# One planner for projection pieces and results, by the latest half each allows

## The chip, the cores and the metric

One NeuronCore of a Trainium2 chip runs the whole kernel. The metric is the device time of one execution in microseconds; three executions of the kernel before gave 4173.58, 4173.59 and 4175.78 us, median 4173.59 us. Everything is float32 except the row maxima that are turned into bfloat16 triples.

## The reference

The input x is (4, 2048, 512). It is layer-normalized to xn; the output is x plus an attention over xn plus a top-1 mixture of experts over xn.

```python
qkv = x @ w_qkv                                   # 512 -> 3 x 512
q, k = spectral_filter(q), spectral_filter(k)     # rfft over the 32 head entries, mask, irfft
scores = einsum('bhqd,bhkd->bhqk', q, k) / sqrt(32)
out = einsum('bhqk,bhkd->bhqd', softmax(scores), v)   # 16 heads, 2048 queries, 2048 keys
attention = out.reshape(B, S, 512) @ w_out + b_out
# experts: each token picks argmax of softmax(xn @ w_gate); the first 100 tokens of each of 8
# experts get gate * (xn @ w_expert + b_expert), all others nothing
x + attention + experts
```

The spectral filter is linear, so it is folded into the weights of q and k once at the start. Attention over 4 x 16 heads of 2048 x 2048 scores is nearly all of the work.

## The kernel before

The work is cut into 16 groups `k` (batch k // 4, four heads each), a group into 4 blocks `n` of 512 queries, a block into 16 *halves* `j` of 128 keys. There are 1024 halves, numbered h = 64 k + 16 n + j; the place of a half in its block is h mod 16. Two halves are a window. The main loop goes through the halves in order, and every engine's instructions keep the order in which they are written (class `InOrder`, whose line 82 is why nearly all instructions of the profile carry L82).

Each half does the same base work:

- TensorE computes two pieces of scores for the *row maxima*, which run 21 halves ahead (`max_matmuls`, four PSUM banks of 128x512 a half, profile name `array<-keys,q`), and the scores themselves by adding the difference between neighbouring key tiles to what PSUM still holds (`scores`, `array<-q,steps_of_keys`).
- ScalarE exponentiates the four score banks in two instructions into the tiles `even` or `odd`.
- VectorE reduces the four banks of the maxima (`max_reduce`, `part<-array`). The first two banks always take one instruction each; the last two take one common instruction if the half's planned cost is above zero, and two otherwise (the argument `u == 0 or not costs[...]` in the main loop).
- TensorE multiplies the *previous* half's exponentials by v (`products`, `array<-even,v` and `array<-odd,v`), and VectorE adds the result to `num`.
- GpSimd and a DMA that accumulates add the exponentials of pairs of halves for the row sums, once a window.

After `products` the half runs its *agenda*: a list of further steps that was planned before the loop. What stands there:

- **Pieces**: `query_key` and `value` compute q, k and v of the next group, 128 tokens at a time: 48 pieces for a group, each 32 matmul instructions of 128 columns (`array<-xnT,w` for q and k, `array<-w,xnT` for v) and one ScalarE copy to q, keys or v. The first piece after a block of maxima is complete also carries the transpose of those maxima (`max_turn`).
- **Closing a block** (`close_steps`): at 5 halves after a block's end a `fold` of row sums on TensorE, at 6 to 13 one of eight reciprocals each on VectorE (`invert`), at 14 a GpSimd product `ot`, then four `result` steps (8 matmuls against w_out each, copied to y by ScalarE, or added to b_out by VectorE in groups with k mod 4 = 0), then `add`, a GpSimd-issued DMA that accumulates 1 MB of y into the output. Before, the results stand at 17, 18, 19, 20 and `add` at 21 halves after the block's end, always.
- **Weight loads** (`load_qkv_weights`): the three weight tiles of the next-but-one group, one buffer each for q, k and v, so each load stands one half after the last piece that uses the old weights. SyncE issues them.
- In the last group of a batch (k mod 4 = 3, except the last) the next batch's tokens: loads of x into `xs`, 16 normalizations on ScalarE (`xs<-xs`), 16 `turn` steps (transposes on TensorE and a ScalarE copy to xnT), then the routing of the tokens to experts (`plan_route`). In group 13 the experts themselves (`place_experts`).

Costs in the plan are counted in pieces: a piece, a result or a fold is 1, a turn 0.5, an expert step up to 5 (`at`, line 927).

Before, the pieces of group k + 1 are placed by `spread` (line 931) within group k alone. It takes an order written out by hand (`projections`, line 468, with two groups named in `CROWDED`), and looks for the lowest even level of cost at which the order fits into the group's 64 halves. The results are already in `costs`, at their fixed halves, and `spread` fills around them as an accumulated sum. The k pieces have an earliest half (the old keys must have been read, `SPENT`, line 1066) and a latest one (the maxima of the next group read them), passed as `latest`.

Of the kernel before, what the change touches and what calls it, by code (L numbers as in the profile page):

```python
# [26 lines left out]
NT = S // P  # L27
# [13 lines left out]
WIN = 2  # L41
NW = NT // WIN
MAX_AHEAD = 42
CROWDED = (1, (B - 1) * NG + 2)


def shape_constants():
# [54 lines left out]
def attention_and_top1_experts(ctx: ExitStack, tc: tile.TileContext, a: dict, out: bass.AP):  # L102
# [304 lines left out]
    def load_qkv_weights(k, s):  # L407
        wg[k, s] = weights.tile([P, NR, P], F32, name=f"w{s}", bufs=1)
        cols = slice(2 * DM + k % NG * P, 2 * DM + (k % NG + 1) * P)
        on.sync.dma_start(out=wg[k, s], in_=w_qkv[:, :, cols] if s == 2 else wd[k % NG][:, :, s, :])  # L410
# [54 lines left out]
        on.scalar.copy(vs[k][:, n * TQ + first : n * TQ + last, :], done)  # L465
        max_store(turned)

    def projections(k, tiles=1, kinds=None):

        kinds = [] if kinds is None else kinds  # L470

        if k == 0:
            order = [(query_key, 0, 1), (query_key, 0, 0)]
            order += [(query_key, n, 1) for n in range(1, NQ)] + [(query_key, 1, 0)]
            order += [(value, n) for n in range(NQ)] + [(query_key, n, 0) for n in range(2, NQ)]
        else:
            first = 2 if k in CROWDED else 3 if k % NG == 0 else 4
            queries, vals = ([(f, n, *s) for n in range(NQ)] for f, *s in ((query_key, 0), (value,)))
            news = [(query_key, n, 1) for n in range(NQ)]
            if first == 4:  # L480
                order = vals + queries[:2] + news + queries[2:]
            else:
                order = vals[:first] + queries[:1] + news[:3]
                order += vals[first : first + 1] + news[3:] + vals[first + 1 :] + queries[1:]
        kinds.extend((2 if f is value else at[1]) for f, *at in order for t in range(0, TQ, tiles))
# [221 lines left out]
    def close_steps(k, n):  # L707

        b = k // NG
        held = {}  # L710

        def fold():
            held["den"] = work.tile([P, QB], F32, tag="den", name="den", bufs=1)
            held["factor"] = work.tile([P, QB], F32, tag="factor", name="factor", bufs=1)
            on.scalar.copy(held["den"], row_sums(ended[k, n][1]))

        def invert(i):
            at = slice(i * PART, (i + 1) * PART)
            on.vector.reciprocal(held["factor"][:, at], held["den"][:, at])

        def divide():
            held["ot"] = work.tile([P, QB], F32, tag="ot", name="ot", bufs=1)
            engine = on.vector if (k, n) == (B * NG - 1, NQ - 2) else on.gpsimd
            engine.tensor_tensor(held["ot"], ended[k, n][0], held["factor"], ALU.mult)

        def result(t):
            if t == 0:
                held["y"] = chunk("y")
            if k % NG == 0:
                on.vector.tensor_tensor(held["y"][:, t, :], project(k, held["ot"], t), b_out, ALU.add)  # L730
            else:
                copy = on.vector.tensor_copy if k == B * NG - 1 and n > 0 else on.scalar.copy
                copy(held["y"][:, t, :], project(k, held["ot"], t))

        def add():
            on.gpsimd.dma_start(out=o[b, n], in_=held["y"], accum_op=ALU.add)

        if (k, n) == (B * NG - 1, NQ - 2):
            steps = [(5, 2, fold)] + [(6 + i // 3, 0, invert, i) for i in range(QB // PART)]
            steps += [(9, 0, divide)]  # L740
            first = 10
        else:
            steps = [(5, 1, fold)] + [(6 + i, 0, invert, i) for i in range(QB // PART)]
            first = 17
            heads[(k * NQ + n + 1) * HB + 14].append(divide)
        steps += [(first + t, 1, result, t) for t in range(TQ)]
        return steps + [(first + TQ, 0, add)]

    def close_last(k, n, num, tiles, y):

# [180 lines left out]
    def spread(steps, last, latest={}):  # L931


        base = steps[0][1]

        def places(level):
            half, done, found = base, costs[base], []
            for place, (cost, first, _) in enumerate(steps):
                stop = latest.get(place, last + 1)
                while half < stop and (half < first or done + cost / 2 > level * (half - base + 1)):  # L940
# [8 lines left out]
        found = next(filter(None, (places(level / 32) for level in range(16, 400))))  # L949
        for (cost, _, step), half in zip(steps, found):  # L950
            at(half, step, cost=cost)
        return found

    stage = {}

# [3 lines left out]
    def in_stage(which, *args):  # L959
        stage["all"][which](*args)  # L960
# [28 lines left out]
    def plan(k):  # L989
# [1 line left out]
        b, c = divmod(k, NG)  # L991
        start = k * GH

        def after_keys_are_spent():

            for i, place in enumerate([j for j, s in enumerate(kinds) if s == 1]):
                cost, _, step = steps[place]
                steps[place] = cost, start + SPENT + i // TQ * TQ, step
                latest[place] = start + SPENT + i // TQ * TQ + 3 * TQ - 1
# [7 lines left out]
        last = start + GH - 1  # L1007
        steps, kinds, latest = [], [], {}
        if k == 0:
            done = spread([(1, 0, step) for step in first_projections_left], 15)  # L1010
            for s in range(3):
                at(done[-1] + 1, load_qkv_weights, 1, s)
            plan_route(20, lambda i: first_route[i]())
            ready = done[-1] + 3
        if c == NG - 2 and b + 1 < B:

            at(start + 20, begin_stage, b + 1)
# [10 lines left out]
        pieces = projections(k + 1, kinds=kinds)  # L1028
        if c == NG - 1:

            late = {8: 9, 12: 14}
            order = [("turn", i) for i in range(8)] + pieces[:4] + [("turn", i) for i in range(8, 12)]
            order += pieces[4:8] + [("turn", i) for i in range(12, NT)] + pieces[8:]
            kinds = [None] * 8 + kinds[:4] + [None] * 4 + kinds[4:8] + [None] * 4 + kinds[8:]
            steps, first = [], start + 1
            for step in order:
                if isinstance(step, tuple):
                    i = step[1]
                    steps.append((0.5, start + late[i] if i in late else 0, lambda i=i: in_stage(4, i)))
                else:  # L1040
                    steps.append((1, 0, step))
            steps[0] = (0.5, first, steps[0][2])
            after_keys_are_spent()
            done = spread(steps, last, latest)
            turned = {i: done[order.index(("turn", i))] for i in range(NT)}
            for i in range(NT):
                at(turned[i] - 1, in_stage, 3, i)
# [3 lines left out]
        else:  # L1051
            steps = [(1, ready if k == 0 else start, step) for step in pieces]
            after_keys_are_spent()
            done = spread(steps, last, latest)
        assert done[-4] >= start + 3 * HB and done[-8] >= start + 2 * HB
        places = [[h for h, s in zip(done, kinds) if s == kind] for kind in range(3)]
        for i, h in enumerate(places[1]):
            assert SPENT <= h - start - i // TQ * TQ < SPENT + 3 * TQ
        assert places[0][3] < start + GH - MAX_AHEAD // 2 and places[0][7] < start + GH + HB - MAX_AHEAD // 2
        for n in range(NQ):  # L1060
            at(start + GH - 10 + n * TQ, key_steps, n)
        if k + 2 < B * NG:
            for s in range(3):
                at(places[s][-1] + 1, load_qkv_weights, k + 2, s)

    SPENT = GH - HB - MAX_AHEAD // 2 + TQ
    ROUTE = len(first_route)
# [12 lines left out]
    place_experts((B - 1) * NG * GH)  # L1080
    for k in range(B * NG):
        plan(k)

    FINAL = (B * NG * NQ - 1) * NW
    LEFT = 3
# [154 lines left out]
```

## Time and profile before

The profiled execution took 4171.94 us, of which 4170.1 us are the span from the first to the last instruction of the program.

| what | value |
|---|---|
| median of three runs | 4173.59 us |
| profiled execution, its span | 4171.94 us, 4170.1 us |
| TensorE matmul busy | 4135.3 us (99%) |
| VectorE busy | 3421.8 us (82%) |
| GpSimd busy | 3010.8 us (72%) |
| ScalarE busy | 2490.8 us (60%) |
| granted TensorE clock | 0.999 of full speed |
| reduces of one bank (128x512) | 2162, 685 ns each |
| reduces of two banks (128x1024) | 967, 1217 ns each |

Engine busy time is the union of instruction intervals. Matmuls overlap one another and their ends are modelled, so two matmul intervals can touch although the array waited between them; the distance between the *starts* of neighbouring groups of matmuls is safer. In this text the length of a half is the distance from the start of its `products` matmuls to the start of the next half's; the agenda of a half lies inside its own length. `PE` is TensorE's matmuls, `DVE` VectorE, `ACT` ScalarE, `POOL` GpSimd, `SP` SyncE.

### The profile page before, as it was taken

What the parts mean: (1) busy time and instruction counts of PE and PEld (TensorE: products, weight loads), DVE (VectorE), ACT (ScalarE), POOL (GpSimd) and SP (SyncE); (2) the same over time, 40 slices, a digit from 0 to 9 for tenths busy, and PEclk for the clock granted to TensorE, in tenths of its full rate; (3) what the DMA queues carried; (4) which work ended last, traced back from release to release, by engine and by line L of the source; (5) the groups of instructions that cost most, each with busy time, mean ns of one, the idle gap of its engine ahead of it and who ended that gap; (6) DMA issues with size and microseconds to landing.
All of it is one profiled execution on the core that took longest, in us unless ns stands there. A gap on an engine that the chain in (4) does not pass through costs nothing.

```text
span 4170.1 us, 121446 instructions
## 1 busy us (share of the span) xinstructions
PE 4135.3 (99%) x52824; PEld 1839.8 (44%) x52824; DVE 3421.8 (82%) x4940; ACT 2490.8 (60%) x3430; POOL 3010.8 (72%) x2102
## 2 busy tenths in 40 slices
PE   8999999999999999999999999999999999999999
PEld 5444444444444444444444444444444443444432
DVE  7778888977888888897788888888778888788895
ACT  4555556676665566657565556566656555556665
POOL 1578776776876777776778767767678776677887
PEclk9999999999999999999999999999999999999999
DMA  3677878987788788899778787899877986778787
GB/s 123 141 154 151 168 149 170 219 195 145 146 164 159 152 161 159 193 198 195 140 149 162 158 160 151 163 198 202 173 154 146 182 159 134 151 160 170 152 169 154
DMA packets 178415, 680.78 MB, mean 163 GB/s; under 512 B 23430, under 2 KB 53288, under 8 KB 113112
## 3 DMA queue, kind: packets, MB, share of 16 engines
q0 software_dynamic: 109856, 601.63, 74.0%
q1 hardware_dynamic: 67952, 71.34, 5.2%
q8 instruction: 414, 6.78, 0.6%
q14 instruction: 121, 0.99, 0.1%
q10 hardware_dynamic: 72, 0.03, 0.0%
HBM read 71.07 MB, written 87.91 MB: 38 GB/s over the span
## 4 chain that ended last, share of the span: by engine, by line
PE 94%; DVE 4%; ACT 1%; issue 1%; DMA 0%; SPq 0%; ACTq 0%
PE array L82 94%; DVE part L82 3%; DVE num L82 1%; ACT odd L82 0%; DVE factor L82 0%; DMA odd<-in_L_attn_w_qkv_dram 0%; DMA w<-in_L_attn_w_qkv_dram 0%; ACT even L82 0%; ACT keys L82 0%; SPq L82 0%; DVE stats L82 0%; DVE y L82 0%; ACT xnT L82 0%; ACT xs L82 0%; SPq L177 0%
## 5 line engine op out<-in xcount | busy, mean ns | idle before, releaser
L82 DVE TENSOR_REDUCE part<-array 128x1 f32<-128x512 f32 (+1 forms) x3129 | 2484.4, 850 | 667.6 <-PE array L82 662.8
L82 POOL TENSOR_TENSOR even<-even 128x1024 f32<-128x1024 f32 x876 | 2121.2, 2521 | 430.6 <-DMA even<-odd 422.9
L82 PE MATMUL array<-keys,q 32*128 32x512 f32 x8192 | 2059.3, 614 | 15.8 <-DVE part L82 5.8
L82 PE MATMUL array<-q,steps_of_keys 32*128 32x512 f32 x8128 | 2021.2, 615 | 0.1
L82 ACT ACTIVATE odd<-array 128x1024 f32<-128x1024 f32 x1024 | 996.7, 1021 | 472.2 <-PE array L82 403.5
L82 ACT ACTIVATE even<-array 128x1024 f32<-128x1024 f32 x1014 | 984.7, 1021 | 440.7 <-PE array L82 425.7
L82 PEld LDWEIGHTS array<-keys,q 32*128 32x128 f32 x8192 | 771.5, 184 | 580.5 <-DVE part L82 351.6
L82 PEld LDWEIGHTS array<-q,steps_of_keys 32*128 32x128 f32 x8128 | 689.2, 183 | 241.3 <-issue 227.9
L82 POOL DMA_DIRECT2D even<-odd x504 | 463.9, 920 | 336.3 <-ACT odd L82 300.2
L82 DVE TENSOR_TENSOR num<-num,array 128x512 f32<-128x512 f32 x960 | 651.0, 678 | 32.7 <-PE array L82 31.3
L82 PEld LDWEIGHTS array<-xnT,w 128*32 128x32 f32 x16384 | 458.7, 110 | 259.6 <-DVE part L82 177.6
L82 PE MATMUL array<-odd,v 128*32 128x512 f32 x4096 | 545.5, 605 | 0.0
L82 PE MATMUL array<-even,v 128*32 128x512 f32 x4056 | 540.2, 605 | 0.8 <-DVE part L82 0.8
L82 PE MATMUL array<-xnT,w 128*32 128x128 f32 x16384 | 527.4, 273 | 2.8 <-issue 1.7
L82 PEld LDWEIGHTS array<-w,xnT 128*32 128x32 f32 x8192 | 229.8, 110 | 147.8 <-DVE part L82 105.0
L82 DVE RECIPROCAL factor<-den 128x64 f32<-128x64 f32 x504 | 274.7, 546 | 0.0
L82 PE MATMUL array<-w,xnT 128*32 128x128 f32 x8192 | 269.4, 273 | 1.9 <-DMA w<-in_L_attn_w_qkv_dram 1.7
L82 PE MATMUL array<-wo,ot 128*32 128x512 f32 x2048 | 266.1, 592 | 0.0
L82 PEld LDWEIGHTS array<-odd,v 128*32 128x32 f32 x4096 | 80.7, 108 | 387.6 <-DVE part L82 379.8
L82 PEld LDWEIGHTS array<-even,v 128*32 128x32 f32 x4056 | 79.8, 108 | 385.3 <-DVE part L82 380.8
L82 POOL DMA_DIRECT2D out_dram<-y x63 | 87.3, 1385 | 176.9 <-ACT y L82 108.5
L82 ACT COPY q<-array 128x128 f32<-128x128 f32 x256 | 67.9, 265 | 182.1 <-PE array L82 178.3
(152 smaller groups left out, 1529.8 us busy)
## 6 DMA issues: line engine op xcount, KB each, us to landing
even<-odd POOLq DMA_DIRECT2D x504, 1024.0 KB, 8.1
out_dram<-y POOLq DMA_DIRECT2D x63, 1024.0 KB, 9.6
xs<-in_L_attn_x_dram SPq DMA_DIRECT2D x96, 256.0 KB
out_dram<-in_L_attn_x_dram SPq DMA_DIRECT2D x16, 1024.0 KB
w<-wd SPq DMA_DIRECT2D x30, 256.0 KB
w<-in_L_attn_w_qkv_dram SPq DMA_DIRECT2D x16, 256.0 KB
wo<-in_L_attn_w_out_dram SPq DMA_DIRECT2D x16, 256.0 KB
negm<-row SPq DMA_DIRECT2D x192, 4.0 KB
```

What stands on the lines that cost most here:

```text
L82: done = act(*args, **kwargs)
```

## The change

All pieces and results go into four queues (`jobs`): q, k, v pieces and results, each in a fixed order, over the whole kernel. An entry holds the earliest half (`release`), the latest (`stop`), the least distance to the entry before it in its queue, the step, and what is to follow one half later (the weight load after the last piece of a kind, or `add` after the last result). A new planner, `level`, goes through the halves once from first to last. A half whose cost is under 0.6 takes the ready entry with the nearest `stop`. A half that has something already takes more only if an entry's `stop` is this very half, or if a look ahead over 48 halves (`missed`) says that waiting would make an entry late.

So pieces of group k + 1 may now stand in group k + 1 itself: v pieces up to three halves before their product, q pieces of later blocks up to 22 halves before the block. Results may slip by up to 8 halves (by 1 in groups with k mod 4 = 0). `CROWDED`, the order by hand and `latest` go. The first piece of a kind stands at least 5 halves after the last piece of that kind of the group before; the weight load between them stands 4 halves or more ahead of it (3 in group 0, where it stands at half 16 and the first piece at 19). In the last group of a batch `spread` still places the turns, against a template of pieces. Within a half the pieces and results now come after all other agenda steps.

The same steps run with the same operands. The planned cost of the halves is 1152.75 before and after. Halves (of 1024) with a planned cost of 0 or 0.25: 84 before, 33 after; with 2 or 2.25: 130 before, 98 after. The program of the changed kernel has the same instructions on every engine, but for 96 one-bank reduces that become 48 two-bank ones on VectorE.

```diff
-CROWDED = (1, (B - 1) * NG + 2)
...
+            order = [(query_key, n, 0) for n in range(NQ)] + [(query_key, n, 1) for n in range(NQ)]
+            order += [(value, n) for n in range(NQ)]
...
-        steps += [(first + t, 1, result, t) for t in range(TQ)]
-        return steps + [(first + TQ, 0, add)]
+        results = [lambda t=t: result(t) for t in range(TQ)]
+        if k == B * NG - 1 and n > 0:
+            steps += [(first + t, 1, step) for t, step in enumerate(results)] + [(first + TQ, 0, add)]
+        else:
+            end = (k * NQ + n + 1) * HB
+            spare = 1 if k % NG == 0 else 8
+            for t, step in enumerate(results):
+                jobs[3].append((end + first, end + first + t + spare, 5 if t == 0 else 1, step, add if t == TQ - 1 else None))
+        return steps
...
+    jobs = [[] for _ in range(4)]
+
+    def level(first, last):
+
+        done = [[] for _ in jobs]
+
+        def ready(half, placed):
+
+            found = []
+            for q, (queue, before) in enumerate(zip(jobs, placed)):
+                if len(before) < len(queue):
+                    release, stop, gap, *_ = queue[len(before)]
+                    if half >= release and (not before or half >= before[-1] + gap):
+                        found.append((stop, q))
+            return min(found, default=None)
...
+        for half in range(first, last):
+            load = costs[half]
+            while found := ready(half, done):
+                stop, q = found
+                if load >= 0.6 and stop > half:
+                    if load > 1.8:
+                        break
+                    tried = [before + [half] if p == q else before for p, before in enumerate(done)]
+                    if missed(half, tried) >= missed(half, done):
+                        break
+                done[q].append(half)
+                load += 1
+        for queue, found in zip(jobs, done):
+            assert len(queue) == len(found)
+            for (release, stop, gap, step, then), half in zip(queue, found):
+                assert half <= stop, (half, stop)
+                at(half, step, cost=1)
+                if then:
+                    at(half + 1, then)
...
-            ready = done[-1] + 3
+            ready = done[-1] + 4
...
+        stays = (k + 1) % NG == NG - 1 and b + 1 < B
+        for s in range(3):
+            for i in range(NT):
+                n = i // TQ
+                if s == 0:
+                    stop = start + GH - MAX_AHEAD // 2 - 1 + n * HB
+                    release = start + 1 + n * HB
+                elif s == 1:
+                    release = start + SPENT + n * TQ
+                    stop = release + 3 * TQ - 1
+                else:
+                    release, stop = start + 1, start + GH + i - 2
+                if stays:
+                    stop = min(stop, start + GH - 1)
+                load = None
+                if i == NT - 1 and k + 2 < B * NG:
+                    load = lambda s=s, k=k: load_qkv_weights(k + 2, s)
+                jobs[s].append((max(release, turned[i] + 2), stop, 0 if i else 5, pieces[s * NT + i], load))
...
+    level(1, END - GH + 3 * HB)
```

More of the change, by code (lines that the diff above doesn't have):

```diff
@@ L466, in value, with projections @@
         max_store(turned)
-    def projections(k, tiles=1, kinds=None):
-        kinds = [] if kinds is None else kinds
+    def projections(k, tiles=1):
         if k == 0:
@@ L476, in projections @@
         else:
[L477 to L485, printed above, removed]
+            order = [(query_key, n, 0) for n in range(NQ)] + [(query_key, n, 1) for n in range(NQ)]
+            order += [(value, n) for n in range(NQ)]
         return [
@@ L929, in at, with missed, spread @@
         costs[half] += cost
-    def spread(steps, last, latest={}):
+    jobs = [[] for _ in range(4)]
[9 more added lines that the diff above has]
+            return min(found, default=None)
+        def missed(half, placed):
+            placed, late = [list(before) for before in placed], 0
+            for later in range(half + 1, half + 3 * HB):
+                for queue, before in zip(jobs, placed):
+                    while len(before) < len(queue) and queue[len(before)][1] < later:
+                        before.append(later)
+                        late += 1
+                if later < last and costs[later] < 0.6:
+                    found = ready(later, placed)
+                    if found:
+                        placed[found[1]].append(later)
+            return late
+        for half in range(first, last):
[17 more added lines that the diff above has]
+                    at(half + 1, then)
+    def spread(steps, last):
         base = steps[0][1]
@@ L937, in places @@
             half, done, found = base, costs[base], []
-            for place, (cost, first, _) in enumerate(steps):
-                stop = latest.get(place, last + 1)
-                while half < stop and (half < first or done + cost / 2 > level * (half - base + 1)):
+            for cost, first in steps:
+                while half < first or done + cost / 2 > level * (half - base + 1):
                     half += 1
@@ L947, in places @@
             return found
[L949 to L952, printed above, removed]
+        return next(filter(None, (places(level / 32) for level in range(16, 400))))
     stage = {}
@@ L992, in plan @@
         start = k * GH
[L994 to L999, printed above, removed]
         if k == 0:
@@ L1006, in plan @@
         at(start + GH // 2, load_out_weights, k + 1)
-        last = start + GH - 1
-        steps, kinds, latest = [], [], {}
+        ready = start + 1
         if k == 0:
-            done = spread([(1, 0, step) for step in first_projections_left], 15)
+            done = spread([(1, 0)] * len(first_projections_left), 15)
+            for half, step in zip(done, first_projections_left):
+                at(half, step, cost=1)
             for s in range(3):
@@ L1027, in plan @@
                 at(start + GH - 6 + i, in_stage, 7, i)
-        pieces = projections(k + 1, kinds=kinds)
+        turned = [ready - 2] * NT
         if c == NG - 1:
             late = {8: 9, 12: 14}
[L1032 to L1047, printed above, removed]
+            kinds = [0] * 8 + [1] * 4 + [0] * 4 + [1] * 4 + [0] * 4 + [1] * 40
+            steps, i = [], 0
+            for kind in kinds:
+                steps.append((1, 0) if kind else (0.5, start + late.get(i, 1)))
+                i += not kind
+            turned = [half for half, kind in zip(spread(steps, start + GH - 1), kinds) if not kind]
+            for i, half in enumerate(turned):
+                at(half, in_stage, 4, i, cost=0.5)
+                at(half - 1, in_stage, 3, i)
             for i in range(2 * TQ, NT):
@@ L1050, in plan @@
             plan_route(turned[NT - 1] + 2, follow_route)
[L1051 to L1059, printed above, removed]
+        pieces = projections(k + 1)
+        stays = (k + 1) % NG == NG - 1 and b + 1 < B
[16 more added lines that the diff above has]
+                jobs[s].append((max(release, turned[i] + 2), stop, 0 if i else 5, pieces[s * NT + i], load))
         for n in range(NQ):
             at(start + GH - 10 + n * TQ, key_steps, n)
-        if k + 2 < B * NG:
-            for s in range(3):
-                at(places[s][-1] + 1, load_qkv_weights, k + 2, s)
     SPENT = GH - HB - MAX_AHEAD // 2 + TQ
```

## The prediction

> **What bounds the kernel now.** I read the page first, then the groups of instructions with shapes kept apart, then three windows, then the timeline of single halves. The page says TensorE, nearly alone:
>
> ```profile
> span 4170.1 us, 121446 instructions
> ...
> PE 4135.3 (99%) x52824; PEld 1839.8 (44%) x52824; DVE 3421.8 (82%) x4940; ACT 2490.8 (60%) x3430; POOL 3010.8 (72%) x2102
> ...
> PE 94%; DVE 4%; ACT 1%; issue 1%; DMA 0%; SPq 0%; ACTq 0%
> ```
>
> Taken at its word, nothing can be won by moving work. But these intervals overlap, so the 99% also holds waits. The groups give what VectorE has to do in a half:
>
> ```profile
> L82 DVE TENSOR_REDUCE part<-array 128x1 f32<-128x512 f32 x2162 | 1385.2, 685 | 654.1 <-PE array L82 650.6
> L82 DVE TENSOR_REDUCE part<-array 128x2 f32<-128x1024 f32 x967 | 1175.8, 1217 | 13.5 <-PE array L82 12.3
> L82 DVE TENSOR_TENSOR num<-num,array 128x512 f32<-128x512 f32 x960 | 651.0, 678 | 32.7 <-PE array L82 31.3
> L82 DVE RECIPROCAL factor<-den 128x64 f32<-128x64 f32 x504 | 274.7, 546 | 0.0
> ```
>
> The windows are four halves with one piece each, three with none, and two with two:
>
> ```profile
> 388.53:403.72 15.19, 15.19 (x229) 7.16 (x225) 14.13 (x22) 8.81 (x13) 10.39 (x8) 1.00 0.79 161
> 3970.34:3980.51 10.17, 10.03 (x76) 3.56 (x73) 10.17 (x19) 6.09 (x7) 5.28 (x5) 1.00 1.07 218
> 3582.40:3591.75 9.35, 9.35 (x181) 5.26 (x177) 6.96 (x11) 5.00 (x9) 4.34 (x3) 1.00 1.10 218
> ```
>
> (Columns: length, busy PE, PEld, DVE, ACT, POOL, granted clock, DMA share, GB/s.) A half is 3.80, 3.39 and 4.67 us long. The second piece costs 0.873 us, the first only 0.41. Without a piece DVE is busy for 10.17 of 10.17 us: TensorE waits for banks. The timeline shows it in the starts:
>
> ```profile
> 388.52 1.06 PE L82 MATMUL array<-even,v 128*32 128x512 f32 x8
> 389.41 1.06 PE L82 MATMUL array<-w,xnT 128*32 128x128 f32 x32
> 392.32 1.07 PE L82 MATMUL array<-odd,v 128*32 128x512 f32 x8
> ...
> 3970.34 1.07 PE L82 MATMUL array<-even,v 128*32 128x512 f32 x8
> ...
> 3973.73 1.06 PE L82 MATMUL array<-odd,v 128*32 128x512 f32 x8
> ```
>
> So TensorE's own line is 2.925 us + 0.873 per piece or result (3.798 - 0.873 = 2.925), plus 0.20 at place 11 (the transposed maxima; 3.997 with one piece) and 0.12 at place 15 (the next block's opening; 3.915). I laid this line beside the lengths of all halves from 1 to 1001, with the plan's content of each. But for the waits below, one-piece and two-piece halves lie on it within 0.02 us, with reciprocals or without; empty ones lie 0.3 to 0.7 us above it. The chain of waits hides this, since it counts such a half as PE. The rest above the line is a few waits at fixed places, of which two are shown here:
>
> ```profile
> 163.31 1.06 PE L82 MATMUL array<-odd,v 128*32 128x512 f32 x8
> 166.12 1.08 PE L82 MATMUL array<-w,xnT 128*32 128x128 f32 x32 [1.74 <-DMA w<-in_L_attn_w_qkv_dram]
> ...
> 572.12 1.93 PE L82 MATMUL array<-xnT,w 128*32 128x128 f32 x64
> 574.44 0.70 PE L82 MATMUL array<-keys,q 32*128 32x512 f32 x2 [0.39 <-ACT keys L82]
> ```
>
> The Trainium skill ("Perfetto Trace Analysis", Identifying the Most-Contended Engine) says matmul busy share is a poor measure because matmuls are pipelined. By the page's 99% the change would be worth nothing, by the lengths of halves what follows; here they agree that the busy share misleads.
>
> **The change part by part.** All matmuls stay, so TensorE's line adds to the same sum; only its waits can change.
>
> *Empty halves filled.* Laying both plans on the line: 71 halves between 1 and 1001 lie in the trace, or would by the 3.39 floor, above the line for want of filler; after, 20. Of the 52 that get a piece or result, 34 lasted 3.27 to 3.54 us (14.92 above the line), 14 at places 10 and 11 lasted 3.60 to 3.69 (7.59), and 4 between expert steps 3.09 to 3.45 (0.70). Gain: 14.92 + 7.59 + 0.70 = 23.2 us. The pieces that fill them leave two-piece halves and are paid on the line either way. One half (18) becomes empty: +0.0 to +0.47 (3.39 - 2.925), I take 0.3.
>
> *The first weight wait.* Half 18 lasted 5.748 us for 3.798: 1.95 us, of which the row shows 1.74. The next first piece is now a q piece at 19, one half later, and q's weights were issued first of the three. Gain 1.95; at worst nothing.
>
> *Keys read in the next half.* The second row above: k pieces at place 54 of a group, maxima read those keys in 55, and TensorE waits for ScalarE's copy. Each of 10 such halves lasted 5.126 for 4.671. After, three remain (halves 54, 310, 566): 7 x 0.455 = 3.2 us gained. Every other q, k or v piece after the change stands three halves or more ahead of its reader.
>
> *Backlog after an empty half.* The halves 128, 320, 384, 576 and 640 follow an empty one and lasted 4.267 for 3.798. Their predecessors are filled: 5 x 0.469 = 2.35 us.
>
> *Turns.* Eight turns now stand two to a half at 193 to 196 (and 449, 705) of three groups. A half then has on ScalarE two exponentials (1.94 together in the timeline), two normalizations (1.56) and two copies (1.11), 4.61 us, against 2.925 + 2 x 0.75 = 4.43 on TensorE (a turn beside a result lengthened its half from 3.784 to 4.551). Excess 0.18 x 3 x 3 = 1.6 us; by unoverlapped durations (2 x 1.021 + 2 x 0.817 + 2 x 0.591 = 4.86) up to 5. Before, the crowded halves 197 to 199 and their likes lay 1.3 us above the line over the three groups. I take +1, bounds -1.3 and +4. The x loads for these normalizations stay put; in SyncE's order two weight loads now stand among the first eight of them, q's behind the fifth and v's behind the seventh, each waiting for the half before it; the tile of the eighth is needed two halves later, some 9 us.
>
> *Results and `add`.* A result is 8 matmuls and a 585 ns ScalarE copy, or 687 ns on VectorE where k mod 4 = 0. There four results run alone in a row: DVE needs 2 x 685 + 1217 + 678 + 687 = 3.95 us against 3.80, and every second such half lasted 3.946. Where a piece stood beside, that was covered; I take +0.5 us. `add` (1.39 us of POOL issue, 9.6 us to landing) moves from place 5 to places 5 to 13, past other POOL issues; POOL has 10.39 of 15.19 us busy in the one-piece window, and y is written again 5 halves (19 us) later at the earliest. Nothing. If that cover went, POOL's sums would hold an `even` buffer and ScalarE with it.
>
> *Reduces.* 96 of 685 ns become 48 of 1217: 7.3 us less on VectorE, none of it on the path once a piece is in the half. Its work there (2 x 685 + 1217 + 678 + 546 = 3.81 with a reciprocal) is at the edge, but the one-piece window shows DVE with 14.13 of 15.19 and halves at 3.798.
>
> *Weight loads.* They wait on SyncE for the last old piece, and after them stand the maxima's rows for the next block, which have several halves. Fourteen are now followed by the first piece that needs them 4 halves later (11 of q, 3 of v); before, the least after group 0's was 7. Four halves are at least 15.2 us. In the trace the packets of 41 such loads end 2.8 to 14.8 us after the issue, median 7.5: no wait, by 0.4 us in the worst pairing. Cost nothing, bounds 0 and 5. [...]
>
> *Routing* of the tokens moves 4 halves earlier with its POOL steps and indirect DMAs; its waits (0.753 and 0.575 us at two halves of each of three groups, two of 1.02 in group 0) go with it. Nothing, bounds -6 and +4.
>
> Sum: -23.2 + 0.3 - 1.95 - 3.2 - 2.35 + 1 + 0.5 = -28.9 us. The profiled execution took 4171.94 (1.84 outside the span), so 4143.0; it lies 1.65 under the median of 4173.59, against which the forecast is 4144.7, rounded to 4145 us (-0.69%).
>
> **The rivals.**
>
> *The weights come too late (slower).* A piece that waits for its weights holds all of TensorE. For: 14 loads with 4 halves, and packets ending at 14.8 us. Against: the longest stood beside x loads or lay elsewhere; the median is half the margin. The change loses once the 14 are late by 28.9 / 14 = 2.1 us on average, that is landing at 17.3 us; at 20 us each it would be 14 x 4.8 = 67 - 29, so 4212 us.
>
> *TensorE is the bound and nothing moves (same).* For: 99%, and equal matmuls. Against: the 3.39 us halves. Time 4173.
>
> *Gains kept, new waits beside them.* The turns cost 4 to 5, routing 4, and some loads 4: 4145 + 3 + 4 + 4 = 4156 us, range 4152 to 4164.
>
> *More than that.* Routing's waits vanish (3 x 1.33 + 2 x 1.02 = 6.0) and the turns' too (2.3): 4137 us.
>
> **How the numbers follow.** Forecast 0.66 (own range 4139 to 4151), new waits 0.15, more 0.06, no change 0.06, late weights 0.07. The range 4135 to 4164 takes in the first three, 0.87, and the bounds of the turns, loads and routing. About 0.2% (8.3 us) is what a measurement here tells from no change: faster, below 4165.2, 0.87; within it 0.06; slower 0.07.
>
> **What would show it.** Right: halves of 3.80 us in a row where 3.39 and 4.67 alternated; only some 20 halves under 3.6 us before the last 21, in group 15 and at the heads of groups; two-bank reduces up by 48; the wait on w at 166 us gone and no new PE wait on w; PE's wait on ACT keys in three places. PE busy falls by about the gain although its matmuls stay. Wrong: PE waits on DMA w near halves 91, 150 or 279, halves of more than 4.9 us at 193 to 196, or one-piece halves longer than 3.85 us in long runs, which would mean VectorE's edge decides.

## The result, and the profile after

The kernel became slower by a little: 4185.22 us, median of 13 runs (4181.02 to 4190.12), against 4175.05 us, median of 13 runs of the kernel before (4172.47 to 4176.77). The ratio is 1.0025, 95% interval 1.0017 to 1.0033. The forecast was 4145 us with a range of 4135 to 4164, so the time lies outside it, on the other side of the kernel before. The profiled execution took 4190.12 us, the longest of the 13; its span is 18.1 us longer than that of before, some 8 us more than the medians show (10.2 us). All sums below are made against that span, so they show somewhat more loss than a typical run has.

The page of the kernel after, its span, its busy times and its chain by engine (the work that ended last, followed back from the last instruction to what released each step):

```profile
span 4188.2 us, 121336 instructions
...
PE 4148.7 (99%) x52824; PEld 1841.5 (44%) x52824; DVE 3423.8 (82%) x4892; ACT 2488.2 (59%) x3430; POOL 3009.3 (72%) x2102
...
PE 93%; DMA 3%; DVE 2%; POOL 1%; issue 1%; ACT 0%; SPq 0%; POOLq 0%; ACTq 0%
```

The matmuls are as many as before, and yet PE is "busy" for 13.4 us longer: intervals of waiting matmuls count as busy. What is new stands in the chain: DMA has 3% where it had 0%, and POOL, which was not in the list, 1%; DVE fell from 4% to 2%. The change did what it says, as the groups of the kernel after with shapes kept apart show:

```profile
L81 DVE TENSOR_REDUCE part<-array 128x1 f32<-128x512 f32 x2066 | 1329.4, 686 | 658.6 <-PE array L81 653.6 <-issue 1.3
L81 DVE TENSOR_REDUCE part<-array 128x2 f32<-128x1024 f32 x1015 | 1234.5, 1218 | 18.3 <-PE array L81 17.5
```

The two-bank reduces are up by 48 and the one-bank ones down by 96. A window over a stretch of the last group that held empty halves before (columns: length, busy PE, PEld, DVE, ACT, POOL, granted clock, DMA share, GB/s) shows a DVE that is no longer busy all the time (9.39 of 10.10 us, where it was 10.17 of 10.17):

```profile
3983.80:3993.90 10.10, 10.10 (x112) 4.05 (x116) 9.39 (x16) 6.64 (x9) 8.69 (x6) 1.00 0.78 157
```

The halves 968 to 970 in this stretch were empty and lasted 3.39, 3.39 and 3.64 us; each now holds a piece or a result and lasts 3.78 to 3.80 us, on TensorE's line. So the filling is there. What was given back stands in the waits. First the list of waits of the kernel before, lines of GpSimd and ScalarE (engine and tile, what it waited for: us in total, times, longest):

```profile
POOL even L82 <- DMA even<-odd: 431.3, 197, 7.7
...
ACT even L82 <- POOL even L82: 6.2, 8, 1.1
...
ACT odd L82 <- DMA even<-odd: 1.4, 1, 1.4
```

and the same view of the kernel after:

```profile
POOL even L81 <- DMA even<-odd: 480.7, 193, 7.3
...
ACT even L81 <- POOL even L81: 32.5, 18, 2.9
ACT odd L81 <- DMA even<-odd: 12.7, 10, 2.0
...
PE array L81 <- issue: 4.1, 5, 2.0
PE array L81 <- POOL even L81: 2.5, 3, 1.3
...
PE array L81 <- DMA w<-wd: 1.6, 1, 1.6
PE array L81 <- ACT keys L81: 1.5, 4, 0.4
```

GpSimd waits 49 us longer for the DMAs that add `odd` to `even`. ScalarE waits 45.2 us for the buffers `even` and `odd`, where it waited 7.6 us, and TensorE's matmuls wait for sums of GpSimd, for which the list of before has no line. ("issue" is time in which an engine waited for nothing that the profile shows.) Seven of the eleven waits on keys went, as foreseen; one wait on weights is new.

To place these, I laid TensorE's line (2.925 us a half + 0.873 for each piece or result, with the floor of 3.39 us for empty halves) under all halves of each profile and summed what lies above it, by stage:

| us above TensorE's line | before | after |
|---|---|---|
| halves 192 to 211, 448 to 467, 704 to 723 (turns) | 1.6 | 20.2 |
| halves 212 to 245 of these groups (routing) | 3.7 | 7.3 |
| halves 31 and 32 of all groups | 0.8 | 6.0 |
| halves 800 to 862 (experts) | 1.7 | 4.3 |
| last group, last 21 halves included | -0.1 | 6.1 |
| first group, with what comes ahead of it | 4.6 | 3.5 |
| all others | 8.3 | 14.1 |
| sum | 20.6 | 61.4 |

(Sums of unrounded numbers.) The plan on the line is 22.6 us shorter, the waits are 40.8 us longer: 18.2 us, against 18.1 in the spans.

### The profile page after: what moved, and what is told of

Read it like the earlier page. It is cut to its first block, busy times and chain, and to the rows that moved or that the text cites. A ratio compares the mean times of both kernels' runs of the same rounds, so it can differ in the third digit from the quotient of the medians.

```text
span 4188.2 us, 121336 instructions
## 1 busy us (share of the span) xinstructions
PE 4148.7 (99%) x52824; PEld 1841.5 (44%) x52824; DVE 3423.8 (82%) x4892; ACT 2488.2 (59%) x3430; POOL 3009.3 (72%) x2102
## 4 chain that ended last, share of the span: by engine, by line
PE 93%; DMA 3%; DVE 2%; POOL 1%; issue 1%; ACT 0%; SPq 0%; POOLq 0%; ACTq 0%
PE array L81 93%; DMA even<-odd 2%; DVE part L81 2%; POOL even L81 1%; DMA w<-wd 0%; DMA xs<-in_L_attn_x_dram 0%; DMA odd<-in_L_attn_w_qkv_dram 0%; ACT xs L81 0%; DVE num L81 0%; ACT odd L81 0%; ACT num L81 0%; POOL steps_of_keys L81 0%; DVE factor L81 0%; ACT even L81 0%; ACT y L81 0%
## 5 line engine op out<-in xcount | busy, mean ns | idle before, releaser
L81 POOL DMA_DIRECT2D even<-odd x504 | 487.2, 969 | 418.5 <-ACT odd L81 369.8
L81 ACT COPY keys<-array 128x128 f32<-128x128 f32 x256 | 67.9, 265 | 186.1 <-PE array L81 173.3
L81 ACT COPY v<-array 128x128 f32<-128x128 f32 x256 | 67.9, 265 | 178.8 <-PE array L81 170.0
```

Source lines behind the costliest of these rows:

```text
L81: done = act(*args, **kwargs)
```

## Where the time went: one DMA in GpSimd's order

GpSimd does its instructions in order. In each window it issues one DMA that adds the 1 MB of `odd` to `even`, and one window later, two after the pair itself, it sums such results over the windows; the sum waits for the DMA. The first window of a block has nothing to be added to, so two windows later, in the block's third, GpSimd has no such sum. These are the halves at places 4 and 5. The timeline of the kernel before on GpSimd (columns: start, length, engine, line, operation, tiles, count, idle time before and what ended it), around such a window, which starts at 1394.1 us:

```profile
1387.33 4.68 POOL L82 TENSOR_TENSOR even<-even 128x1024 f32<-128x1024 f32 x2 [1.94 <-DMA even<-odd]
...
1393.19 0.85 POOL L82 DMA_DIRECT2D even<-odd  x1
1397.21 1.31 POOL L82 DMA_DIRECT2D out_dram<-y  x1 [3.17 <-DVE y L82]
1399.68 0.87 POOL L82 DMA_DIRECT2D even<-odd  x1 [1.17 <-ACT odd L82]
1400.34 4.91 POOL L82 TENSOR_TENSOR even<-even 128x1024 f32<-128x1024 f32 x2
1408.34 0.86 POOL L82 DMA_DIRECT2D even<-odd  x1 [3.09 <-ACT odd L82]
1412.40 4.67 POOL L82 TENSOR_TENSOR even<-even 128x1024 f32<-128x1024 f32 x2 [3.19 <-DMA even<-odd]
```

From 1392 to 1400 us there is no sum over windows. `add` (`out_dram<-y`) lies in that gap: GpSimd was idle for 3.17 us before it, for 1.17 us after it and for 3.09 us before the pair after that, each time waiting for VectorE or ScalarE, so it was ahead of them. The sum for the pair issued right behind `add`, at 1399.68 us, starts 12.7 us later and waits 3.19 us. Before the change 62 of the 63 adds stand at place 5, by half mod 16. After it 39 have moved: 1 to place 6, 13 to 7, 4 to 8, 10 to 9, 3 to 10 and 8 to 13. The same view of the kernel after, with `add` at half 439, place 7:

```profile
1856.31 1.36 POOL L81 DMA_DIRECT2D out_dram<-y  x1
1857.19 1.42 POOL L81 DMA_DIRECT2D even<-odd  x1
1857.77 5.53 POOL L81 TENSOR_TENSOR even<-even 128x1024 f32<-128x1024 f32 x2
1862.41 1.72 POOL L81 DMA_DIRECT2D even<-odd  x1
1871.43 2.37 POOL L81 TENSOR_TENSOR even<-even 128x1024 f32<-128x1024 f32 x1 [7.30 <-DMA even<-odd]
```

In both kernels 1 MB of y stands directly in front of 1 MB of `odd`, and that pair is slow in both: in the trace of before, where 52 such pairs have a recorded landing, it landed 12.5 us after its issue (median), the pairs not close behind an `add` after 7.7 us. What is new is the place. Sums stand on both sides, GpSimd has no idle time before `add`, and the sum that waits for the pair keeps it idle for 7.30 us. The chain that ended last, asked for 1855 to 1916 us of the kernel after (start, length, what), goes through that DMA instead of through TensorE:

```profile
1856.36 0.83 POOL out_dram L81
1857.19 14.09 DMA even<-odd
...
1878.88 9.40 DMA even<-odd
...
1908.17 2.35 POOL even L81
```

GpSimd is then late, and the windows of one-piece halves (7.6 us) hold too little spare time to make it up at once: the stretch of two such windows before had POOL busy for 10.39 of 15.19 us, which leaves 4.80 us. The late sums hold buffers, and ScalarE waits for these. ScalarE of the kernel after before and in half 193 (from 864.0 us), whose length is 7.38 us for 4.40:

```profile
852.59 1.94 ACT L81 ACTIVATE even<-array 128x1024 f32<-128x1024 f32 x2 [2.27 <-POOL even L81]
...
860.95 1.94 ACT L81 ACTIVATE even<-array 128x1024 f32<-128x1024 f32 x2 [2.88 <-POOL even L81]
...
865.23 1.94 ACT L81 ACTIVATE odd<-array 128x1024 f32<-128x1024 f32 x2 [0.94 <-DMA even<-odd]
```

or a `fold` on TensorE needs the late sums itself, as in half 453, which lasted 7.01 us for 3.78:

```profile
1908.25 1.05 PE L81 MATMUL array<-even,ones 128*32 128x512 f32 x4 [0.73 <-POOL even L81]
1910.56 1.05 PE L81 MATMUL array<-even,ones 128*32 128x512 f32 x4 [1.25 <-POOL even L81]
```

The largest excess of a single half, 4.7 us in half 708, has another last link: a turn there waits for a load of x that took 18.25 us in the chain. Why it took so long is not shown; without `add` (a run below) the half lasts 4.25 us, and with the results fixed, where it holds one turn and one result, 4.55.

All this was read from traces. The runs below test it.

## The experiments

The ratio of each run is to runs of the kernel before on the same chip; its medians stand beside (4170.52, 4176.06 and 4171.70 us for the three groups of four runs).

### Results back at their places; the turns one to a half

Edit of the first, to the kernel after:

```diff
-        if k == B * NG - 1 and n > 0:
+        if True:
             steps += [(first + t, 1, step) for t, step in enumerate(results)] + [(first + TQ, 0, add)]
```

> The changed kernel with the results back at halves 17 to 20 and add at 21 after a block's end; pieces and turns as in the changed kernel (planned anew around them). Theory A (the turns, two to a half, make most of the new waits): within 4 us of the changed kernel's 4185. Theory B (moving the results moves add, and its 1 MB collides with the DMAs that add pairs of exponentials): the new waits outside the turns go, 10 to 15 us, so 4170 to 4175. Theory C (the even filling by itself makes windows of 7.6 us, too short for a pair's DMA and its sums): 4185.

Measured: 4162.07 us against 4170.52, ratio 0.9980 (0.9970 to 0.9989). Against the changed kernel's 1.0025 that is 0.0045, about 19 us (14 to 24 by both intervals). The turn stage fell from 20.2 to 2.6 us above the line, ScalarE's waits for GpSimd from 32.5 to 12.5 us. Theory B had put 10 to 15 us on it, from outside the turns; the turn stage recovered as well. So pieces by due time gain (8 us against the kernel before), and freeing results and `add` loses more than that.

The second edit, to the kernel after, plans at most one turn beside other work:

```diff
-                steps.append((1, 0) if kind else (0.5, start + late.get(i, 1)))
+                steps.append((1, 0) if kind else (1, start + late.get(i, 1)))
...
-                at(half, in_stage, 4, i, cost=0.5)
+                at(half, in_stage, 4, i, cost=1)
```

> The changed kernel with a turn counted as 1 instead of 0.5, so that turns stand one to a half again, and the normalizations and x loads with them; results as in the changed kernel. Theory A: 12 to 18 us less than the changed kernel, 4167 to 4173, and halves 192 to 211 of group 3 and their likes near TensorE's line. Theory B: 4185 less at most 3. Theory C: 4185.

Measured: 4193.27 us, ratio 1.0052 (1.0036 to 1.0069). With a lighter turn stage the kernel is not faster; the plan, which shifts the results again, now puts 16 adds at place 7 and 11 at place 13. The third run has both edits:

> Both edits: results back at their old halves and one turn to a half; only the pieces are levelled. Theories A and B together: the gain of 28 us that was forecast appears, 4150 to 4160. Theory A alone: 4167 to 4173. Theory B alone: 4170 to 4175. Theory C: 4185.

Measured: 4162.71 us, ratio 0.9980 (0.9970 to 0.9990), the same as with the first edit alone. Two turns in a half are not the cause, although the halves with them are where most of the loss shows.

### `add` left out, after and before

Edit, to the kernel after and to the kernel before:

```diff
         def add():
-            on.gpsimd.dma_start(out=o[b, n], in_=held["y"], accum_op=ALU.add)
+            return
```

> The changed kernel without the add DMAs of the 63 blocks: the attention of those blocks is not added to the output. Theory B: the collisions go with them, at least 10 us less than 4185, and ScalarE's waits for even and odd buffers (32.5 and 12.7 us) fall to the 6 us of the kernel before. Theory A: 4185 less at most 5, the turn stage keeps its waits. Theory C: 4185 less at most 5, with the same waits for even.

Measured in the kernel after: 4153.68 us against 4170.52, ratio 0.9958 (0.9944 to 0.9972), 28 us less than with `add`. The results slip as in the changed kernel, so it is `add` that costs, not the results. The turn stage is at 2.3 us. The list of waits of this run:

```profile
POOL even L81 <- DMA even<-odd: 245.9, 140, 6.9
...
ACT even L81 <- POOL even L81: 3.6, 4, 1.4
```

> The kernel before without the add DMAs of the 63 blocks: the attention of those blocks is not added to the output. Theory B1: add costs nearly nothing in its old place, so 4171 less at most 4. A theory that add loads the DMA engines wherever it stands: as much less as the changed kernel without it, 30 us, 4141.

Measured in the kernel before: 4174.70 us against 4176.06, ratio 0.9998 (0.9989 to 1.0008). The same 63 DMAs that cost 28 us in the kernel after, with 39 of them at new places, cost nothing that can be measured at their old places in the kernel before.

### The kernel before with `add` moved

Edit, to the kernel before (2 in place of 4 in the second of the two runs); only `add` moves, by 4 halves to place 9 or by 2 to place 7:

```diff
-        return steps + [(first + TQ, 0, add)]
+        return steps + [(first + TQ + (4 if (k, n) < (B * NG - 1, NQ - 2) else 0), 0, add)]
```

> The kernel before, with one edit: add stands at 25 instead of 21 halves after the block's end (place 9 instead of 5), results and pieces unmoved. Theory B1 (in place 5, the third window of a block, GpSimd has no sum to make, so the DMA of a pair may be late there and nowhere else): each of 62 blocks loses what 39 moved adds lost in the changed kernel, 23 / 39 = 0.6 us, so 4171 + 37, at least 4185. Theory B2 (the results' own matmuls and copies in other halves are to blame): 4171 within 3.

Measured at place 9: 4195.49 us against 4176.06, ratio 1.0045 (1.0030 to 1.0061), +19.4 us, about half of the 37 expected. Only part of it is the expected path: 13.2 us lie in the last 21 halves, and TensorE waits for the maxima's rows as well (list of waits of this run):

```profile
PE array L82 <- DMA negm<-row: 10.9, 5, 3.1
```

> The kernel before with add at 23 instead of 21 halves after the block's end, place 7, where most of the moved adds of the changed kernel stand. If only the window without a sum (places 4 and 5) is free of cost: 4176 + 8 to + 20. If the cost at place 9 came from the maxima's rows, which are sent at places 11 to 14, alone: 4176 within 4.

Measured at place 7: 4233.15 us against 4171.70, ratio 1.0138 (1.0122 to 1.0154), +61.5 us by the medians and far more than expected; 9.1 us of it lie in the last 21 halves. Its list of waits:

```profile
POOL even L82 <- DMA even<-odd: 604.9, 216, 9.9
...
ACT even L82 <- POOL even L82: 72.8, 39, 4.2
...
ACT odd L82 <- DMA even<-odd: 27.5, 12, 4.8
```

All pieces and results of this kernel stand as before. One DMA a block, two halves later, takes GpSimd's waits for its pairs from 431 to 605 us and ScalarE's for buffers from 7.6 to 100 us. This is the cause by itself, larger than in the change. The price depends on the place: 61.5 / 62 = 0.99 us for an `add` at place 7, 19.4 / 62 = 0.31 at place 9, and nothing at place 5. The change's 13 adds at place 7 would come to 13 x 0.99 = 13 us, and if the other 26 cost what they do at place 9, all 39 to 13 + 26 x 0.31 = 21 us. This is an estimate, and a rough one: the price at place 9 comes for two thirds from the last 21 halves, and places 6, 8, 10 and 13 were not tried. It is of the size of the 19 us of the first experiment and the 28 of the fourth.

### Most of GpSimd's sums left out

Is it GpSimd that must catch up, or the DMAs that are in each other's way? This edit keeps every DMA at its place and leaves out most sums (610 of GpSimd's 2102 instructions), to the kernel after:

```diff
-                    if 0 < w and (window < FINAL - LEFT or last and w < NW - 4):
+                    if 0 < w and (w > 5 or window > FINAL - 2 * NW) and (window < FINAL - LEFT or last and w < NW - 4):
```

> The changed kernel without the GpSimd sums of the second to sixth pair of every block but the last; the row sums leave these keys out. If add costs by way of GpSimd (its sums wait in order for a pair's DMA that stands behind the 1 MB of add, and the buffers come free late): the cost of 23 to 31 us goes, at most 4162. If the DMAs behind add hold up the buffers and loads directly: 4180 or more.

Measured: 4153.76 us against 4171.70, ratio 0.9956 (0.9941 to 0.9971). That is as fast as without `add`, with `add` where the change puts it. ScalarE no longer waits for `even` of GpSimd at all; the list of waits of this run keeps

```profile
POOL even L81 <- DMA even<-odd: 183.8, 71, 7.3
...
ACT odd L81 <- DMA even<-odd: 3.7, 2, 2.3
```

So `add` costs through the sums behind it in GpSimd's order, and not by slowing transfers for everybody: these stay, and the sums that are left still wait up to 7.3 us for a pair. Whether it is the late GpSimd or the buffers that its sums hold, this run can't tell apart. The same with the results at their old places:

> The control to the run before: results and add in their old halves, pieces levelled, and the same sums left out. If sums do not matter where add stands at place 5: 4162 less at most 5. If leaving sums out speeds the kernel whatever add does: the same gain as in the run before.

Measured: 4154.92 us, ratio 0.9960 (0.9945 to 0.9975): without the sums, the place of `add` makes no difference, 0.9956 and 0.9960; with them it made the 19 us of the first experiment. The control shows one thing more. Against that experiment (0.9980), with `add` at place 5 in both, leaving the sums out is worth some 8 us, with 1 to 16 by both intervals. So in the more evenly filled kernel the sums cost something even with `add` at its old place, and that part of the gain of leaving them out isn't owed to its move. A part of it, 1.7 us, is half 91, which waits for weights and lasts 5.74 us in the first experiment, and 4.00 here. The 8 us are also of the size of the 9 us between the first experiment and the fourth; a run with the results fixed and no `add`, which would tell, was not made.

### The rest of the missing gain, and a faster kernel

With `add` out of the way (fourth run), the span is 17.2 us shorter than before (4152.9 against 4170.1), not 28.9. Its sum above the line is 26.1 us, where before has 20.6. Three stages are larger: routing 7.3 (before 3.7), experts 4.3 (1.7) and the halves 31 and 32 of the groups 4.5 (0.8). For routing I suspected the order inside a half: pieces were ahead of the routing's steps before and are behind them after the change. Edit, on top of the first experiment:

```diff
-            for (release, stop, gap, step, then), half in zip(queue, found):
+            for (release, stop, gap, step, then), half in reversed(list(zip(queue, found))):
                 assert half <= stop, (half, stop)
-                at(half, step, cost=1)
+                agenda[half].insert(0, step)
+                costs[half] += 1
```

> The first experiment (results and add in their old halves, pieces levelled) with the pieces ahead of all other agenda steps of a half, not behind them. If the place within the half matters (a piece behind a routing step or a fold waits for the bank or the sums that these wait for): the halves 85, 277, 533 and 789 and the routing halves lose 5 to 8 us of waits, 4154 to 4158. If not: 4162.

Measured: 4156.44 us against 4176.06, ratio 0.9954 (0.9940 to 0.9967). Routing fell from 9.1 to 5.0 us, and the turn stage from 2.6 to 0.2. Most of the fall in routing lies in halves 230 and 236 and their likes, which hold a piece and a routing step: 5.22 and 4.83 us in the first experiment, 4.37 and 4.44 here, as in the kernel before. The order within the half was worth some 11 us against the first experiment by the ratios (0.9954 against 0.9980); the two profiled spans, 4161.2 and 4154.7 us, differ by 6.5.

Next, one half more between k pieces and their readers and between weights and their first piece, on top of this:

```diff
-                    stop = release + 3 * TQ - 1
+                    stop = release + 3 * TQ - 2
...
-                jobs[s].append((max(release, turned[i] + 2), stop, 0 if i else 5, pieces[s * NT + i], load))
+                jobs[s].append((max(release, turned[i] + 2), stop, 0 if i else 6, pieces[s * NT + i], load))
```

> The same, with each k piece at least two halves ahead of the half that reads its keys, and 6 halves instead of 5 between the last piece of a kind and the first of the next group. Fifteen halves that waited 0.455 us for a copy go (6.8 us), and the wait of 1.7 us for q's weights; seven more halves stay empty (3.1 us): 5 us less than the run with pieces first. If late copies and weights did not count: 3 us more.

Measured: 4154.75 us, ratio 0.9947 (0.9933 to 0.9960), not to be told from the run before it. TensorE's waits on keys fell from 6.2 us in 16 places (first experiment) to 0.4 us in one. The last run takes back the second line of this edit (5 halves again):

> The run with more slack, but with 5 halves again between the last piece of a kind and the first of the next group: no more empty halves than the changed kernel. The seven empty halves are worth 3.1 us, the weights' wait 1.4: 4153, 1 to 2 us under it.

Measured: 4149.85 us against 4171.70, ratio 0.9947 (0.9934 to 0.9961), the shortest median of all, with the same ratio as the run before it, and 22 us under the kernel before. Its page and, below it, its list of waits:

```profile
span 4148.0 us, 121300 instructions
...
PE 96%; DVE 3%; DMA 1%; issue 0%; ACT 0%; SPq 0%; POOL 0%; DVEq 0%; POOLq 0%
```

```profile
ACT even L81 <- POOL even L81: 14.9, 13, 2.0
...
PE array L81 <- DMA w<-wd: 3.1, 2, 1.6
```

GpSimd's own waits for pair DMAs are 457.5 us in this run, more than the 431.3 of before, so their total by itself is no measure of the loss. Two waits on weights are left, 3.1 us; the extra half for them bought nothing in the ratio. This version keeps the change's planner for the pieces, with the results and `add` where they were, the pieces first in a half, and k pieces one half earlier.

## Why the prediction was wrong

**The step that failed** is *Results and `add`*, where the move of `add` from place 5 past other POOL issues was costed as "Nothing". The reason given was POOL's 10.39 busy of 15.19 us, an average over four halves that says nothing of the order in which GpSimd comes to its waits. The next sentence named the mechanism, "POOL's sums would hold an `even` buffer and ScalarE with it", but priced it neither in the sum nor in the range. It measured 19 us (results and `add` back) to 28 us (`add` out). The trace of before could have told: the missing sum at places 4 and 5 was to be seen in GpSimd's timeline, and GpSimd's waits for pair DMAs (431.3 us, 197 times) stood in the list of waits as the largest of its own. Of the 40 us between forecast and measurement, `add` is then 28 by the fourth run; most of the rest stands below, under *Routing* and under what was not in the sum.

The other steps:

- *Empty halves filled*, -23.2: right. Of the 52 halves 48 lie on TensorE's line; the 52 together lost 20.2 of their 23.2 us above it, and what is left is nearly all in halves 222, 478 and 734, 1.0 us each. Under 3.6 us there are 16 halves between 1 and 1001 after, where there were 57.
- *The first weight wait*, -1.95: right; half 18 went from 5.748 to 3.426 us.
- *Keys read in the next half*, -3.2: right; three such halves are left, the three named (54, 310 and 566), at 4.25 us. Half 118, which held two pieces and now holds a single step, went from 5.126 to 3.783.
- *Backlog after an empty half*, -2.35: right; the five halves went from 4.267 to 3.798.
- *Turns*, +1 with bounds -1.3 and 4: right in itself, since the stage has 2.3 us above the line without `add` and 2.6 with results fixed, against 1.6. With the late sums the same stage lost 18.5 us.
- *Weight loads*, 0 with bounds 0 and 5: one of the loads was late, and half 91 lasted 5.76 us for 4.00. SyncE issued its weights at 436.24 us, 4.5 us after GpSimd had issued an `add`, and the piece waited until 455.9, 19.6 us later, where the longest of the loads before had taken 14.8. That `add` had not been moved away from place 5, and with the results fixed half 91 lasts 5.74 us as well; without any `add`, or without most sums, it lasts 4.00. So the wait comes from `add` near the load, not from the move of `add`.
- *Routing*, "Nothing, bounds -6 and +4": +3.6, in the bounds. Halves 222, 226 and 232 and their likes lie 1.0 us above the line each; the same routing steps, four halves later in the kernel before, cost 0.8, 0.6 and 0.6. For 226 and 232 it is the piece behind the routing's step: with results fixed these steps stand at 230 and 236 and cost 1.4 and 1.0, and with the pieces first 0.6 each.
- *Reduces*, nothing on the path: nothing in the runs speaks against it.
- Not in the sum: the halves 31 and 32 of groups, where two q or k pieces stand in one half (+5.2 us in this profile), and the experts (+2.7). TensorE waits with "issue" in three of the former, halves 288, 415 and 800, for 1.9 us in all; of the 4.1 us in the list 2.0 lie in the first 25 us of the kernel, where before had 1.7. The first varies in the other runs (0.0 to 4.5 us); the cause of neither is settled.

Two of the signs of being wrong appeared, a wait on w at half 91 and half 193 with 7.38 us, and both are gone without `add` (4.00 and 4.25 us). Of the rivals, the one on the slower side blamed late weights; they gave 1.8 us of the 40.8. *New waits beside them* is what happened in kind, but its price of 11 us came from turns, routing and loads, and none of these was the large one. That TensorE is the bound and nothing moves is refuted by the last run, 22 us faster with the same matmuls and 99% busy throughout. Its gain is 7 us short of the 28.9 that were forecast for the pieces.

## What to carry to other kernels

An engine that takes its instructions in order has places that are free and places that are not, and its busy share does not tell them apart: before a DMA or an instruction is moved to another place in its order, find what stands behind it there, and what that waits for. A place that looks arbitrary, such as always 21 halves after a block, can be free where its neighbours are not; moving that step alone in the old kernel takes one run and would have shown it. A planner that balances one engine's work should carry as fixed whatever another engine's order depends on.

## What the runs showed of the hardware that was not expected

- In the kernel before, the price of one 1 MB accumulating DMA on GpSimd's queue goes from nothing to 0.99 us of the whole kernel's time, by two halves (some 7.6 us) of shift, and falls again to 0.31 us two halves later. It is not monotonic in the delay. The pair right behind it lands late at the free place too (12.5 us against 7.7); there GpSimd had idle time to spare.
- A load of 256 KB, issued 4.5 us behind such a DMA, took 19.6 us until its reader could start.
- The time of the changed kernel scatters over 9 us in 13 runs, that of before over 4 us. That the late sums cause this is likely and was not tested.
